# Making the inner sums of the image for q and k of the second pair on VectorE instead of loading them

## The chip, the cores and the metric

One core of one Trainium2 chip. The metric is the device time of one execution in microseconds (us), the median of several executions.

## The reference, cut to what matters

An attention block on x of shape (16, 512, 32, 32), fp32, four heads of 128 channels, 1024 positions:

```python
    xn = group_norm(x, 8 groups) * gamma + beta
    qkv = jnp.einsum('oc,bchw->bohw', qkv_w, xn) + qkv_b[:, None, None]
    q, k, v = jnp.split(qkv, 3, axis=1)
    # ... to heads ...
    attn = jax.nn.softmax(jnp.einsum('bhnd,bhmd->bhnm', q, k) * scale, axis=-1)
    out = jnp.einsum('bhnm,bhmd->bhnd', attn, v)
    # ... back to channels ...
    out = jnp.einsum('oc,bchw->bohw', proj_w, out) + proj_b[:, None, None]
    return x + out
```

## The kernel before

The products for q, k, v and the projection are two-level Strassen products (7 of 8 block products, twice). The inner level needs four sums of image blocks, t1 to t4, for each of four groups of outer products. The image is the same for the first pair of heads, for v and for the second pair, so before made the sums once ("keep": made on VectorE, stored to DRAM) and loaded them twice ("load"):

```python
            def load(h, m):
                if sums == "load" and h < len(OUTER):
                    nc.sync.dma_start(sum_tile(h, m), inner_kept[b, h, m])

            def inner_sum(m):
                if sums == "load":
                    return
                sum_tile(g, m)
                a, c = {
                    "t1": ("b12", "b11"), "t2": ("b22", "t1"), "t3": ("t2", "b11"),
                    "t4": ("b21", "t2"),
                }[m]
                for i in range(n):
                    nc.vector.tensor_sub(have[m][:, i, :], inner(i, a), inner(i, c))
                if sums == "keep":
                    ...  # stored by GpSimd's queue
```

Scores (s), exponentials (p) and the weighted sum (po) of one head run beside one such product. In head 0 of a batch that is q and k of the second pair, in head 1 the projection of the batch before, in head 2 q and k of the first pair of the next batch, in head 3 its v. The softmax denominators of the head before are summed on VectorE, their reciprocals written to DRAM as one row and read back broadcast to all partitions, and the division waits for that:

```python
    def denominators(b, h):
        ...
        nc.vector.reciprocal(r, l[:, 3, :])
        row = dpool.tile([1, N], F32, tag="row", name=f"row_{b}_{h}")
        nc.sync.dma_start(row.rearrange("o (c i) -> (o c) i", i=BLK), r)
        rinv[b, h] = lpool.tile([P, N], F32, tag="rinv", name=f"rinv_{b}_{h}")
        nc.sync.dma_start(rinv[b, h], row.to_broadcast((P, N)))
    ...
    def divide(b, h):
        nc.vector.tensor_mul(os_[b, h], os_[b, h], rinv.pop((b, h)))
```

v is transposed through DRAM, by GpSimd's queue: each finished block is written (vd<-vu) and read back in four parts of 128 KB (v<-vd). The last of these reads fall into head 0 of the next batch.

## Time and profile before

| | before |
|---|---|
| median of 3 executions | 3350.72 us (3336.61 to 3360.77) |
| TensorE, VectorE busy | 96%, 75% of the span |
| heads 0, 1, 2, 3, mean of batches 1 to 14 | 56.2, 50.0, 51.2, 49.2 us |
| bytes moved | 589.27 MB |

TensorE is busy almost throughout, so the question is only where it stands. The four kinds of head need about equal matmul work, yet head 0 is 5 to 7 us longer than the others, and the list of waits has one large entry there, on an addition that frees the y bank, the accumulator that the next product needs (L529). That addition stands on VectorE behind the division, and the division waits for the broadcast of the reciprocals. The prediction shows the lines. The view that names the end of that chain is VectorE's list of waits (us in total, times, longest us), of before:

```profile
DVE o L807 <- DMA rinv<-row: 129.0, 36, 9.8
```

### The profile page before, as it was taken

To read this page: it belongs to the slowest core of one execution; us is meant where nothing else is said; L and a number is where in the kernel's file an instruction comes from. 1 tells how busy PE (TensorE), PEld (TensorE's weight loads), DVE (VectorE), ACT (ScalarE), POOL (GpSimd) and SP (SyncE) were. 2 spreads that over 40 slices of the span, in tenths; PEclk is the share of its full clock that TensorE was granted. 3 is DMA by queue.
4 is the path that set the end of the run, shared out by engine and by line. 5 is a ranking of instruction groups with operands and counts; after the bars stand their busy time and mean duration, and the time that the engine had idled before them with its cause. 6 is when DMAs were issued, how large, how long until landed. Compare 5 with 4: busy or idle time off the path is not lost.

```text
span 3343.7 us, 33635 instructions
## 1 busy us (share of the span) xinstructions
PE 3216.1 (96%) x10474; PEld 2183.1 (65%) x10474; DVE 2521.0 (75%) x4161; ACT 1437.4 (43%) x2709; POOL 525.6 (16%) x938
## 2 busy tenths in 40 slices
PE   8999999999999999999999999999999999999999
PEld 6566666666666666666666666666666666666664
DVE  7876868768687776877768677786777868778675
ACT  2534435344353443535435353353534435344342
POOL 1011121111211112120121201212012121121100
PEclk9999999999999999999999999999999999999999
DMA  6665564555645456464564645646456464464731
GB/s 222 218 202 174 171 211 148 180 174 176 214 157 183 156 184 200 160 189 152 178 197 160 193 150 179 211 148 211 141 170 212 154 215 141 162 202 161 219 128 45
DMA packets 209527, 589.27 MB, mean 176 GB/s; under 512 B 32960, under 2 KB 64192, under 8 KB 209344
## 3 DMA queue, kind: packets, MB, share of 16 engines
q1 hardware_dynamic: 140080, 368.89, 34.1%
q0 software_dynamic: 67392, 216.07, 19.2%
q10 hardware_dynamic: 1872, 2.11, 0.2%
q8 instruction: 86, 1.41, 0.2%
q14 instruction: 97, 0.79, 0.1%
HBM read 448.28 MB, written 138.67 MB: 176 GB/s over the span
## 4 chain that ended last, share of the span: by engine, by line
PE 57%; DVE 11%; issue 9%; DMA 9%; POOL 1%; ACT 0%; POOLq 0%; DVEq 0%; SPq 0%; ACTq 0%
PE po L797 16%; PE s L712 15%; PE qk_x L510 6%; PE qk_y L510 5%; PE v_x L510 4%; PE pp_x L510 3%; PE v_y L510 3%; PE pp_y L510 3%; DMA w<-kept 2%; DMA rinv<-row 2%; DMA y<-in_x 2%; DMA row<-r 2%; DVE xt L272 1%; DVE tot L725 1%; DVE vt L649 1%
## 5 line engine op out<-in xcount | busy, mean ns | idle before, releaser
L717 ACT ACTIVATE p<-s 128x512 f32<-128x512 f32 x1024 | 610.1, 596 | 1069.4 <-PE s L712 1063.8
L712 PE MATMUL s<-qk,qk 128*128 128x512 f32 x2048 | 1060.2, 599 | 2.2 <-ACT p L717 1.9
L797 PE MATMUL po<-p,v 128*128 128x512 f32 x2048 | 1058.4, 598 | 1.3 <-ACT o L804 1.3
L797 PEld LDWEIGHTS po<-p,v 128*128 128x128 f32 x2048 | 602.1, 303 | 331.8 <-issue 215.5
L725 DVE TENSOR_TENSOR tot<-tot,p 128x1024 f32<-128x1024 f32 x385 | 469.8, 1220 | 115.2 <-ACT p L717 112.7
L712 PEld LDWEIGHTS s<-qk,qk 128*128 128x128 f32 x2048 | 391.8, 192 | 93.7 <-issue 29.7
L510 PEld LDWEIGHTS qk_x<-qk_t,w 128*128 128x128 f32 x1344 | 251.1, 191 | 180.9 <-issue 71.9
L510 PE MATMUL qk_x<-qk_t,w 128*128 128x256 f32 x1344 | 360.5, 385 | 7.2 <-ACT qk_u L421 5.9
L529 DVE TENSOR_TENSOR qk_r<-qk_y,qk_u 128x512 f32<-128x512 f32 (+1 forms) x256 | 158.8, 620 | 158.3 <-ACT qk_u L421 132.6
L421 ACT COPY qk_u<-qk_x 128x512 f32<-128x512 f32 (+1 forms) x256 | 136.1, 532 | 254.2 <-PE qk_x L510 254.2
L499 POOL DMA_DIRECT2D kept_t<-qk_t x256 | 138.2, 541 | 487.8 <-DVE qk_t L495 439.8
L510 PE MATMUL qk_y<-qk_t,w 128*128 128x256 f32 x448 | 135.5, 418 | 72.4 <-DVE qk_r L529 67.4
L660 POOL DMA_DIRECT2D vd<-vu x120 | 66.3, 552 | 804.6 <-DVE vu L652 780.3
L807 DVE TENSOR_TENSOR o<-o,rinv 128x1024 f32<-128x1024 f32 x63 | 77.0, 1223 | 129.5 <-DMA rinv<-row 129.0
L510 PE MATMUL pp_x<-pp_t,w_proj 128*128 128x256 f32 x630 | 173.3, 389 | 0.0
L510 PEld LDWEIGHTS v_x<-v_t,w_v 128*128 128x128 f32 x630 | 118.4, 190 | 79.1 <-issue 38.3
L697 POOL DMA_DIRECT2D out_y<-y x120 | 66.2, 551 | 652.1 <-DVE y L696 619.8
L529 DVE TENSOR_TENSOR v_r<-v_y,v_u 128x512 f32<-128x512 f32 (+1 forms) x120 | 74.7, 623 | 124.2 <-ACT v_u L421 116.6
L510 PE MATMUL v_x<-v_t,w_v 128*128 128x256 f32 x630 | 166.6, 381 | 0.0
L510 PEld LDWEIGHTS qk_y<-qk_t,w 128*128 128x128 f32 x448 | 87.1, 203 | 113.2 <-DVE qk_r L529 73.3
L665 POOL DMA_DIRECT2D v<-vd x240 | 139.9, 590 | 100.6 <-issue 45.2
L510 PEld LDWEIGHTS pp_x<-pp_t,w_proj 128*128 128x128 f32 x630 | 113.9, 190 | 63.7 <-issue 18.9
(204 smaller groups left out, 4358.4 us busy)
## 6 DMA issues: line engine op xcount, KB each, us to landing
w<-kept SPq DMA_DIRECT2D x90, 896.0 KB, 6.3
kept_t<-qk_t POOLq DMA_DIRECT2D x192, 256.0 KB, 2.9
qk_t<-kept_t SPq DMA_DIRECT2D x192, 256.0 KB, 4.6
v_t<-kept_t SPq DMA_DIRECT2D x180, 256.0 KB, 2.7
w_v<-kept_v SPq DMA_DIRECT2D x45, 896.0 KB, 4.9
w_proj<-kept_proj SPq DMA_DIRECT2D x45, 896.0 KB, 4.5
rinv<-row SPq DMA_DIRECT2D x63, 512.0 KB, 4.9
x<-in_x POOLq DMA_DIRECT2D x60, 512.0 KB, 5.6
```

Of the source, the lines that this page charges most:

```text
L421: nc.scalar.copy(t[n][:, :width], t["x"][:, :width])
L499: nc.gpsimd.dma_start(t, have[m][:, :n])
L510: nc.tensor.matmul(acc[:, ts(i, Q)], have["w"][:, i, SLOTS[an], :], inner(i, bn), start=(first and i == 0), stop=True, skip_group_check=True,)
L529: nc.vector.tensor_add(dst, view(a), view(c))
L660: nc.gpsimd.dma_start(rows[which][ts(h, P), :], u)
L665: nc.gpsimd.dma_start(vs[b, pair][ts(q, BLK), half].rearrange("m h (k i) j -> m (h k) (i j)", k=n), rows[which].rearrange("(k m) (q e) -> ...
L697: nc.gpsimd.dma_start(out[b, ts(o, P), ts(half, HALF)], t)
L712: nc.tensor.matmul(sc, ks[b, h][:, ts(j, P)], qs[b, h][:, ts(half, HALF)], start=True, stop=True)
L717: nc.scalar.activation(ps[s][:, ts(half, HALF)], sc, AF.Exp, scale=SCALE)
L725: nc.vector.tensor_add(tot[b, h][:, i], tot[b, h][:, i], ps[s][:, i])
L797: nc.tensor.matmul(po[b, h][:, i], v_block(b, h, j), ps[s][:, i], start=(j == 0), stop=(j == NB - 1),)
L807: nc.vector.tensor_mul(os_[b, h], os_[b, h], rinv.pop((b, h)))
```

## The change

The intent is to spend VectorE's spare time in head 0 in place of loads there. q and k of the second pair make their sums ("make") and store nothing; v alone loads the stored ones.

```diff
         return two_levels(
-            f"qk_{b}_{pair}", pair, b, lambda: xb[b], finish, "load" if pair else "keep"
+            f"qk_{b}_{pair}", pair, b, lambda: xb[b], finish, "make" if pair else "keep"
         )
@@
     next_v, next_qk = [], [qk_groups(0, 1)]
-    ahead["qk_0_1"]()
@@
-                units.append(ahead[f"v_{b + 1}" if h == 2 else f"qk_{b + 1}_1"])
+                if h == 2:
+                    units.append(ahead[f"v_{b + 1}"])
```

## The prediction

> **What bounds the kernel now.** I began with the page of the whole execution, which names the busiest engine, and then cut the span at the first score matmul (s) of each head, because four kinds of head alternate and have different limits. In head 0 of a batch the scores run beside q and k of the second pair (the part that the change touches), in head 1 beside the projection of the batch before, in head 2 beside q and k of the first pair of the next batch, in head 3 beside its v.
>
> ```profile
> PE 3216.1 (96%) x10474; PEld 2183.1 (65%) x10474; DVE 2521.0 (75%) x4161; ACT 1437.4 (43%) x2709; POOL 525.6 (16%) x938
> ```
>
> TensorE is the bound, VectorE (DVE) second at 75%. The table of stretches for batch 7, heads 0, 1, 2, 3, in this order:
>
> ```profile
> core 0: us, PE busy (x) PEld busy (x) DVE busy (x) ACT busy (x) POOL busy (x), PEclk, DMA share, GB/s
> 1487.00:1543.20 56.20, 51.02 (x164) 34.77 (x163) 36.06 (x54) 19.02 (x34) 12.43 (x22) 0.97 0.69 211
> 1543.20:1593.60 50.40, 49.80 (x168) 34.33 (x167) 42.45 (x80) 33.48 (x70) 7.29 (x12) 1.00 0.36 125
> 1593.60:1644.70 51.10, 49.74 (x163) 33.50 (x162) 43.48 (x78) 19.13 (x34) 9.70 (x18) 1.00 0.54 184
> 1644.70:1694.00 49.30, 49.05 (x164) 34.27 (x164) 35.19 (x49) 19.13 (x34) 5.09 (x9) 1.00 0.57 184
> ```
>
> Head 0 is the long one: 56.2 us (14 such heads, batches 1 to 14, sum to 787.3 us, mean 56.2; heads 1, 2 and 3 average 50.0, 51.2 and 49.2). Its clock is below 1.00 and its DMA share is the highest, while its VectorE load is one of the two lowest. All four need about the same matmuls: in the timeline two records of 512 columns start 0.86 us after the two before, and so do four of 256, so 64 and 98 of them take 64 x 0.43 + 98 x 0.215 = 48.6 us. Head 0 thus loses 7.6 us per batch, the others 0.6 to 2.6. The list of TensorE's waits over the span names the loss:
>
> ```profile
> PE qk_y L510 <- DVE qk_r L529: 67.9, 15, 7.9
> PE qk_x L510 <- DMA w<-kept: 18.4, 23, 2.1
> ```
>
> 15 waits, one per batch, mean 4.5 us. The timeline of batch 7, VectorE:
>
> ```profile
> 1494.59 0.17 DVE L739 TENSOR_TENSOR l<-l 32x32 f32<-32x32 f32 x1
> ...
> 1495.46 0.34 DVE L742 RECIPROCAL r<-l 32x32 f32<-32x32 f32 x1
> ...
> 1499.68 1.22 DVE L723 TENSOR_TENSOR tot<-p,p 128x1024 f32<-128x1024 f32 x1 [1.69 <-ACT p L717]
> 1507.62 1.23 DVE L807 TENSOR_TENSOR o<-o,rinv 128x1024 f32<-128x1024 f32 x1 [6.72 <-DMA rinv<-row]
> ...
> 1511.42 0.68 DVE L529 TENSOR_TENSOR qk_r<-qk_y,qk_u 128x512 f32<-128x512 f32 x1
> ```
>
> TensorE:
>
> ```profile
> 1505.73 1.03 PE L510 MATMUL qk_x<-qk_t,w 128*128 128x256 f32 x4
> 1511.56 1.87 PE L510 MATMUL qk_y<-qk_t,w 128*128 128x256 f32 x4 [4.80 <-DVE qk_r L529]
> 1513.22 1.91 PE L712 MATMUL s<-qk,qk 128*128 128x512 f32 x2
> ```
>
> The queue of SyncE (SP):
>
> ```profile
> 1493.23 0.32 SPq L484 DMA_DIRECT2D qk_t<-kept_t  x1
> 1495.83 0.32 SPq L744 DMA_DIRECT2D row<-r  x1
> 1496.25 0.51 SPq L484 DMA_DIRECT2D qk_t<-kept_t  x1
> 1500.77 0.32 SPq L746 DMA_DIRECT2D rinv<-row  x1
> 1501.19 0.86 SPq L484 DMA_DIRECT2D qk_t<-kept_t  x2
> 1504.21 0.32 SPq L350 DMA_DIRECT2D w<-kept  x1
> ```
>
> The chain: reciprocal done at 1495.8; the 4 KB row goes out at once, but the broadcast that reads it is issued only 4.9 us later and lands another 6.8 us later. VectorE stands 6.72 us at the division, and the additions that free the y bank are behind it, so TensorE stands 4.80 us. Then s takes 1.91 instead of 1.02 us: half clock, about 1.8 us more.
>
> **What the Trainium skill says.** (1) "TensorE: Matmul & The Clock Gate", Part 1: after about one idle window of 3.4 us the array drops to half rate, and the window is free-running. The trace agrees (the 1.91 us above), except that in batch 4 an idle of 2.64 us was enough. (2) The same page, on the array and the queue depths: ACT and DVE are strict FIFO; that is why a late broadcast holds additions that are ready. (3) "DMA: Bandwidth & Descriptors", "Issuing engines are not separate DMA queues": SP's and GpSimd's transfers share 16 engines. The trace agrees: in stretches of 4 us the DMA share is 0.97 to 1.05 from 1503 to 1519. (4) "VectorE: DVE Perf Modes", on the errata and the tier table: fp32 tensor_tensor runs at 1x, 58 + 256 cycles at 0.96 GHz, 0.33 us. Records of this form last 0.41 us but start 0.335 us apart back to back, so the cost is the page's.
>
> **The change, part by part.** It removes per batch the 12 loads of 256 KB and 4 of 128 KB of head 0, 3.5 MB, 56 MB of 589. (The stores stay, v loads them.) It adds 28 subtractions per batch:
>
> ```profile
> L495 DVE TENSOR_TENSOR qk_t<-x,qk_t 128x256 f32<-128x256 f32 x128 | 51.6, 413 | 0.6
> ```
>
> 28 x 0.335 = 9.4 us of VectorE per batch, 150 us in all. Head 0 goes from 36.1 to about 46 us of VectorE, against 43.5 in head 2, which makes the same sums today and loses 2.6 us.
>
> Now TensorE's path in head 0, with the order of the changed kernel on batch 7's times. *First wait.* One t1 subtraction comes ahead of the last v outputs, in a stretch where VectorE has no gap: it delays the end of v by 0.33 us. The second t1 stands behind L739: it starts at 1494.65 and ends at 1495.07. TensorE, which now takes s between the two halves of that product, wants it at 1493.46: 1.6 us lost. The two t2 follow behind the small transpose and behind the reciprocal, ending at 1495.6 and 1496.3, where a full TensorE would have needed them earlier: with the restart the product with t2 ends at 1496.8 and not 1494.75, so 2.05 us are lost. No single idle reaches 2.6 us, so I expect no clock drop. *Division.* The reciprocal moves only to 1495.55. Without the two loads around it I put the row at 2.5 us (over the trace the row lands in 2.1 by the median, and here the v transfers still run) and the broadcast at 5 us (median 4.9): landing at 1504. VectorE reaches the division at 1502.3, after the first tot, and has 1.13 (it) + 0.67 (two t4) + 1.25 (two L272) + 1.2 (two L529) = 4.25 us until the bank is free, 1508.3. TensorE, 2 us late, arrives at 1508.0. So 0.3 us, in place of 4.8, and no half clock. *Weights of group 2.* Their load (w) is issued when group 0 ends (1505.4) and needed 6.3 us later. In head 2 they land in 5.5 to 6.1, in head 0 today in 10.5, hidden by the long wait. With the sums' loads gone but x and residuals still loading, I choose 7: 0.7 us. *Rest* of the head, small releases and restarts: 0.9 us. Sum: 2.05 + 0.3 + 0.7 + 0.9 = 4.0 us, against 7.6: 3.6 us saved.
>
> Total: 15 batches x 3.6 = 54 us; less 15 x 0.33 = 5 at the end of v; less an estimated 2 in batch 0, where head 0 loses only 1.0 today and VectorE gets fuller. Net 47: 3350.7 - 47 = 3304 us, 1.4% faster.
>
> **Rivals.** *A, head 0 becomes head 2*: 51.2 us, 5.0 saved, 75 in all, less 7: 3283 us, just at 2%. For it: same matmuls, same sums. Against: head 0 starts behind v's transposes and a division, and the t2 come late by the order. *B, the wait stays*: v's transfers of GpSimd (eight v<-vd issued from 1499 to 1503) and not the loads keep the broadcast late, while the first wait is added: about 4.8 + 1.8 + 2 remain, 3350 to 3370. For it: engines stay full through v's part even without 3.5 MB. Against: two loads stand in the very queue of row and broadcast. *C, VectorE becomes the bound in head 0*: 46 of 52.6 us is 88%, and single waits for bank y come back; each 2.6 us wait would also cost the clock. That gives 3320 to 3350. Against: heads 1 and 2 run at 85% with 1.4 and 2.6 us of loss, and VectorE idles 20 of 56.2 us in head 0 today.
>
> **Range and chances.** The middle is 3303. Rivals A and C bound it: 3270 to 3338. The threshold of 2% is 3284, only reached if nearly all of A comes true: 0.23. Slower than 3418 needs more than B: 0.03. Within 2%: 0.74.
>
> **What would show it.** Right: head 0 at 52 to 53 us; the list of waits loses the 67.9 us of qk_y on L529 and gains some 25 us of waits on qk_t subtractions; the gap before the division (6.72 us in batch 7) falls to about 2; the clock in head 0 is 1.00; weights wait up to 1 us more per batch. Wrong: row and broadcast as late as now (B), or new waits on L529 through the second half of head 0 (C), or no early wait (A).

## The result, and the profile after

After: 3314.73 us, median of 4 executions (3313.17 to 3319.11), against 3349.2 of before (4 executions, 3336.61 to 3360.77). The ratio is 0.99, 95% interval 0.9863 to 0.9937. Ratios here are the mean time of one kernel's runs over that of the other's of the same rounds, so not quite the ratio of the medians quoted. The kernel is 1.0% faster by the ratio, 34.5 us by the medians.

The page's first part, of after: 448 more instructions on VectorE, 139 us more busy time, TensorE's work unchanged.

```profile
PE 3206.6 (97%) x10474; PEld 2169.8 (65%) x10474; DVE 2659.6 (80%) x4609; ACT 1437.6 (43%) x2709; POOL 525.5 (16%) x938
```

The heads now take 53.98, 50.00, 51.30 and 49.42 us (before 56.22, 50.02, 51.20, 49.25; means of batches 1 to 14, cut at each head's first score matmul in the trace). 14 batches save 14 x 1.99 = 27.9 us; batches 0 and 15 and the start lose 1.5; together the 26.4 us by which the two profiled spans differ (3343.7 and 3317.3). Only head 0 gains. The stretch of head 0 in batch 7 of after (span, busy time of each engine, clock, DMA share, GB/s), whose heading the prediction shows:

```profile
1479.30:1534.30 55.00, 50.97 (x164) 34.58 (x163) 44.61 (x81) 18.95 (x34) 12.43 (x22) 0.97 0.54 161
```

The DMA share fell from 0.69 to 0.54 and VectorE rose from 36.06 to 44.61 us, but the clock is still 0.97. TensorE's waits over the span of after:

```profile
PE qk_y L510 <- DVE qk_r L529: 36.9, 16, 5.1
PE qk_y L510 <- DVE qk_t L495: 29.2, 27, 1.8
PE qk_x L510 <- DMA w<-kept: 11.5, 17, 1.6
```

The wait behind the division was halved (67.9 to 36.9 us), not removed, and a new wait on the subtractions came (qk_t; 22.0 of the 29.2 us in heads 0 of batches 1 to 15). VectorE's list of waits of after:

```profile
DVE o L807 <- DMA rinv<-row: 100.4, 39, 8.7
```

Batch 7 of after shows both waits. VectorE:

```profile
1486.90 0.40 DVE L495 TENSOR_TENSOR qk_t<-x 128x256 f32<-128x256 f32 x1
...
1487.64 0.33 DVE L742 RECIPROCAL r<-l 32x32 f32<-32x32 f32 x1
...
1493.20 1.23 DVE L723 TENSOR_TENSOR tot<-p,p 128x1024 f32<-128x1024 f32 x1 [0.30 <-ACT p L717]
1498.97 1.23 DVE L807 TENSOR_TENSOR o<-o,rinv 128x1024 f32<-128x1024 f32 x1 [4.54 <-DMA rinv<-row]
```

TensorE:

```profile
1487.35 0.70 PE L510 MATMUL qk_y<-qk_t,w 128*128 128x256 f32 x2 [1.46 <-DVE qk_t L495]
...
1502.85 2.07 PE L510 MATMUL qk_y<-qk_t,w 128*128 128x256 f32 x4 [2.57 <-DVE qk_r L529]
1504.72 1.65 PE L712 MATMUL s<-qk,qk 128*128 128x512 f32 x2
```

SyncE's queue, with no load of sums left in it (the last line merges two issues, so its 17.60 us is no transfer time):

```profile
1488.00 0.32 SPq L744 DMA_DIRECT2D row<-r  x1
1490.57 0.32 SPq L746 DMA_DIRECT2D rinv<-row  x1
1497.73 17.60 SPq L350 DMA_DIRECT2D w<-kept  x2
```

GpSimd's queue:

```profile
1487.82 0.54 POOL L684 DMA_DIRECT2D y<-in_x  x1
1488.65 4.06 POOL L665 DMA_DIRECT2D v<-vd  x7 [0.29 <-issue]
1493.21 0.58 POOL L665 DMA_DIRECT2D v<-vd  x1 [0.50 <-DMA v<-vd]
```

In the means of batches 1 to 14 the row now lands sooner (issued 8.73 us into head 0, landed 2.09 us later; before 8.95 and 4.76), so the broadcast is issued 2.9 us earlier, at 10.8 us. But it then takes 8.4 us to land (before 6.6), at 19.2 us into the head (before 20.3). Of the 2.9 us, 1.8 are given back in the transfer. In batch 7 seven reads of v are issued around it and one behind them. The second idle of TensorE there, 2.57 us, again costs the clock: the two s after it take 1.65 us and not 1.02. Of the 14 heads 0, the clock is 1.00 in 6 and 0.97 in 8.

### The profile page after: what moved, and what is told of

It reads as the page before. It is cut to its first block, busy times and chain, and to the rows that moved or that the text cites.

```text
span 3317.3 us, 33461 instructions
## 1 busy us (share of the span) xinstructions
PE 3206.6 (97%) x10474; PEld 2169.8 (65%) x10474; DVE 2659.6 (80%) x4609; ACT 1437.6 (43%) x2709; POOL 525.5 (16%) x938
## 3 DMA queue, kind: packets, MB, share of 16 engines
q0 software_dynamic: 67392, 216.07, 20.3%
## 5 line engine op out<-in xcount | busy, mean ns | idle before, releaser
L510 PE MATMUL qk_y<-qk_t,w 128*128 128x256 f32 x448 | 132.7, 403 | 64.2 <-DVE qk_r L529 34.8
L529 DVE TENSOR_TENSOR qk_r<-qk_y,qk_u 128x512 f32<-128x512 f32 (+1 forms) x256 | 158.7, 620 | 41.7 <-ACT qk_u L421 22.0
L529 DVE TENSOR_TENSOR v_r<-v_y,v_u 128x512 f32<-128x512 f32 (+1 forms) x120 | 74.8, 623 | 124.8 <-ACT v_u L421 117.1
L510 PEld LDWEIGHTS pp_x<-pp_t,w_proj 128*128 128x128 f32 x630 | 113.8, 190 | 63.9 <-ACT pp_u L421 18.9
L665 POOL DMA_DIRECT2D v<-vd x240 | 139.9, 590 | 53.3 <-issue 44.7
```

The lines of the kernel that those rows point to most:

```text
L510: nc.tensor.matmul(acc[:, ts(i, Q)], have["w"][:, i, SLOTS[an], :], inner(i, bn), start=(first and i == 0), stop=True, skip_group_check=True,)
L529: nc.vector.tensor_add(dst, view(a), view(c))
L665: nc.gpsimd.dma_start(vs[b, pair][ts(q, BLK), half].rearrange("m h (k i) j -> m (h k) (i j)", k=n), rows[which].rearrange("(k m) (q e) -> ...
```

## The experiments

My theory before the first run: the broadcast lands late because the reads of v share the DMA engines with it, and the first wait (on t1) is a loss beside it. The rivals: the first wait alone bounds head 0, or VectorE does. Over all runs I measured the same things in the trace, means of batches 1 to 14:

| kernel | row lands after issue | broadcast lands after issue | lands, us into head 0 | head 0, us | median, us | ratio to before [95%] |
|---|---|---|---|---|---|---|
| before | 4.8 | 6.6 | 20.3 | 56.2 | | |
| after | 2.1 | 8.4 | 19.2 | 54.0 | 3314.73 | 0.99 [0.9863, 0.9937] |
| e1, no sums at all | 3.8 | 6.6 | 19.4 | 55.2 | 3335.88 | 0.9959 [0.9939, 0.9978] |
| e4, division later | 2.1 | 8.1 | 18.9 | 52.2 | 3298.31 | 0.9843 [0.9826, 0.9859] |
| e6, before, division later | 4.7 | 6.4 | 19.9 | 56.7 | 3355.65 | 1.0014 [0.9993, 1.0034] |
| e5, reads of v held | 2.0 | 6.1 | 16.9 | 51.1 | 3280.12 | 0.979 [0.9774, 0.9806] |
| e5 again | 2.1 | 6.1 | 16.9 | 51.0 | 3279.41 | 0.9817 [0.98, 0.9833] |
| e7, before, reads held | 4.3 | 6.3 | 19.5 | 55.6 | 3345.45 | 0.9985 [0.9952, 1.0018] |
| e3, group 0 loaded | 3.7 | 5.6 | 18.1 | 53.5 | 3326.62 | 0.9934 [0.9906, 0.9962] |
| e9, group 0 loaded, reads held | 3.8 | 5.6 | 18.2 | 53.3 | 3324.9 | 0.9919 [0.9895, 0.9943] |
| e10, end of v later | 1.5 | 5.6 | 16.6 | 51.5 | 3277.62 | 0.9808 [0.9791, 0.9824] |
| e11, end of v later, reads held | 1.5 | 5.9 | 17.1 | 51.0 | 3272.99 | 0.9803 [0.9784, 0.9822] |
| e14, reads of c21 held | 1.9 | 7.8 | 18.4 | 52.5 | 3301.21 | 0.9867 [0.9845, 0.989] |
| e15, reads of c12 held | 2.0 | 6.7 | 17.4 | 51.2 | 3277.22 | 0.9798 [0.9775, 0.9821] |

Before ran beside them: 3350.98 us (7 runs) with e1, e4, e5, e6; 3349.67 (9) with e3, e7, e9; 3341.88 (7) with e10, e11 and e5 again; 3342.0 (7) with e14, e15.

### e1_no_sums: neither loaded nor made

The second pair reads raw blocks in place of sums. The result is wrong (relative error 0.10).

```diff
             def inner_sum(m):
-                if sums == "load":
+                if sums == "load" or site == 1:
                     return
@@
             def inner(i, m):
+                if m[0] == "t" and site == 1:
+                    m = {"t1": "b12", "t2": "b22", "t3": "b22", "t4": "b21"}[m]
```

> Wrong result on purpose: the second pair's q and k neither load nor make their inner sums, every product reads raw image blocks instead. My theory: in head 0 the first wait (1.6 us, on the t1 subtraction) goes, but TensorE then reaches the held y bank about 2 us earlier, and the division still stands until the broadcast lands, some 19 us into the head; so the wait on L529 grows from 2.3 to about 4 us per batch, the clock drops in nearly every batch, and the time stays at 3305 to 3320. Rival, that the subtractions cost what their waits show (29 us) on top: about 3285.

Measured: 3335.88 us, slower than after. TensorE's waits of this kernel (its L531 is the addition L529):

```profile
PE qk_y L512 <- DVE qk_r L531: 64.0, 16, 5.2
```

Both times missed, but the mechanism of my theory came: without the first wait TensorE comes to the division earlier, the broadcast lands at 19.4 us (after: 19.2), the wait there is back at 64.0 us, some 4 us per batch, and the clock drops in all 14 heads 0. So removing the first wait gained nothing here; it lies in the shadow of the broadcast. The row took 3.8 us here with no loads of sums left, so these loads are not all that makes it late. It was issued 0.44 us behind a load of the residual in most batches, where after issues it 0.18 us behind; that this is the reason is not shown.

### e4_late_division and e6_before_late_division: the division behind a later addition

In head 0 the division is put behind the running sum of step 3, in after (e4) and in before (e6), so that the additions that free the bank no longer stand behind it.

```diff
                 if half == 0 and j == 5 and s > NB:
-                    divide(*where(s - NB)[:2])
+                    if h == 0:
+                        with tc.issue_after(tot_add[s - 2].ins):
+                            divide(*where(s - NB)[:2])
+                    else:
+                        divide(*where(s - NB)[:2])
```

> The changed kernel with only the division of head 0 moved: VectorE may take it only after the running sum of step 3. My theory: the wait of TensorE on L529 in head 0 (37 us) and the half clock (some 15 us) go, head 0 falls from 54.0 to about 52 us, its clock is 1.00, the time is about 3282 (3274 to 3292). Rival, that another wait (weights of group 2, or VectorE as the bound) takes its place: 3300 or more.

> The kernel before with only the division of head 0 moved as in the run above it. If the held division were all that the change relieved, head 0 would fall from 56.2 to about 50 us and the time to 3255 to 3270, below every kernel that makes the sums. My theory: the loads also keep the weights of group 2 late (10.5 us from issue to landing against 6.3 us until they are wanted), so a wait on these of about 4 us, with half clock after it, comes in its place: 3295 to 3330.

e4: 3298.31 us, between the two expectations. The wait on L529 in head 0 is gone, but the weights of group 2 are met:

```profile
PE qk_x L510 <- DMA w<-kept: 32.5, 28, 2.4
```

e6: 3355.65 us, no gain, and my number missed. But the mechanism of my theory came: nearly all of the wait moved to the weights (66.4 us in heads 0, with half clock in all 14 of batches 1 to 14), which land 10.8 us after their issue while the sums are loaded (counted from the end of the issuing instruction, as are all landings of weights here):

```profile
PE qk_x L510 <- DMA w<-kept: 81.4, 30, 6.3
```

So in before two things lay under the wait, one behind the other, and removing the upper alone gains nothing. In e4 the weights land 6.5 us after their issue, and 16.8 us of waits on them are left in heads 0. Moving the division pays only after the loads of sums are gone.

### e5_v_held: the last eight reads of v wait for the division

```diff
+            if which in ("c21", "c12"):
+                held.append(read)      # the four dma_start of v<-vd, as a function
+            else:
+                read()
@@
     def divide(b, h):
-        nc.vector.tensor_mul(os_[b, h], os_[b, h], rinv.pop((b, h)))
+        ins = nc.vector.tensor_mul(os_[b, h], os_[b, h], rinv.pop((b, h)))
+        while held and h == HEADS - 1:
+            held.pop(0)(ins)           # each read depends on the division
```

> The changed kernel, but the last eight reads of v (v<-vd, GpSimd's queue) wait for the division of head 0. If these eight are why the broadcast takes 8.2 us in head 0, it lands within 5.5 us of its issue, the gap before the division falls from 4.2 to under 1.5 us, the waits on L529 nearly vanish, and the time is about 3288 (3278 to 3300), unless the reads, now later, delay something else. Rival, that residual and image loads or the broadcast itself are slow: landing still 7 us or more, 3310 to 3320.

Measured: 3280.12 us, correct, 0.979: inside the range given, though the landing took 6.1 us and not 5.5. The division in batch 7, and the reads behind it in GpSimd's queue:

```profile
1479.58 1.23 DVE L823 TENSOR_TENSOR o<-o,rinv 128x1024 f32<-128x1024 f32 x1 [1.29 <-DMA rinv<-row]
```

```profile
1481.10 4.65 POOL L668 DMA_DIRECT2D v<-vd  x8 [6.61 <-DVE o L823]
```

The gap before the division is 1.29 us, where after has 4.54. The broadcast lands at 16.9 us, the waits on L529 fall to 3.8 us in all heads 0, and the clock is 0.999. The hold also moves what GpSimd's queue, which runs in order, has behind the reads: the loads of x go out some 10 us later (24.1 us and not 14.6), and loads of the residual earlier. So it is not the reads alone that moved.

### e7_before_v_held: the same hold without the change

The edit of e5, on before.

> The kernel before (sums loaded), with the last eight reads of v held until the division of head 0, as in the run that held them in the changed kernel. If v's reads alone made the broadcast late, the loads would cost nothing once these are held: 3275 to 3290, and the change would be worth nothing on top. My theory: loads and reads of v compete for the same engines in the same 20 us, so either alone keeps the row or the broadcast late: row still lands some 4 us after its issue, division at 18 to 19 us into head 0, waits on L529 of 25 to 50 us over the run, 3305 to 3325.

Measured: 3345.45 us, 0.9985; both expectations missed, mine in size: the waits on L529 stay at 60.3 us and not 25 to 50. The row still lands 4.3 us and the broadcast 6.3 us after their issue. The change alone is worth 35 us, the hold alone about 4 (its interval includes nothing), the two together some 70. With the loads of sums or with the reads of v, either alone, the broadcast stays past 19 us.

### e3_first_loaded and e9_first_loaded_v_held: only group 0 loaded

The sums of group 0 are loaded again at the end of head 3, those of groups 1 to 3 made, so that no subtraction stands ahead of the reciprocal and the first wait goes. e9 has the hold of e5 too. The edit is shown against before, whose loads ahead of group 0 stay:

```diff
-                if sums == "load":
+                if sums == "load" or (sums == "first" and g == 0):
                     return
@@
-            f"qk_{b}_{pair}", pair, b, lambda: xb[b], finish, "load" if pair else "keep"
+            f"qk_{b}_{pair}", pair, b, lambda: xb[b], finish, "first" if pair else "keep"
```

> The changed kernel, but the sums of the first group of the second pair are loaded as before (at the end of head 3) and only those of the other groups made. My theory: the first wait on a subtraction (22 us over the heads 0) goes, but as in the run without sums TensorE comes to the y bank 2 us earlier, while the broadcast lands as late as ever, so the wait on L529 grows to about 60 us and the clock drops in most batches: 3320 to 3338, slower than the changed kernel. Rival, that the first wait is a cost by itself: about 3290.

> As the run with the first group loaded, and the last eight reads of v held until the division. My theory: now that the broadcast lands by about 17 us, nothing stands behind the first wait and its removal counts: head 0 falls from 51.1 us to 49.4 to 50.2, waits on L529 stay under 12 us over the run, 3250 to 3268, faster than every kernel so far. Rival, that the earlier TensorE just meets the division again: 3275 to 3290.

e3: 3326.62 us, inside the range, but with 39.8 us of waits on L529 and not about 60, as the broadcast lands at 18.1 us and not as late as ever. e9: 3324.9 us (5 rounds), a clear miss. The first wait went in both, yet with the reads held the division is met as long as without. Waits of e9:

```profile
PE qk_y L510 <- DVE qk_r L529: 42.7, 16, 4.7
```

With 1 MB of loads at the seam of the two heads the row lands 3.7 us after its issue again, and the whole chain with it (18.2 us). That the loads do it is argued: the order on VectorE changed too, and e1 has a late row without them.

### e10_v_tail_later and e11_v_tail_and_held: the other order at the seam

t1 and t2 of group 0 are made before the denominators' work, and the last additions, writes and reads of v are emitted after it. e10 removes and holds no transfer; e11 adds the hold of e5.

```diff
                 if g == len(OUTER) - 1:
-                    run(pending)
+                    if site == "v":
+                        tail.extend(pending)
+                    else:
+                        run(pending)
                     pending.clear()
@@
         if 0 < s < steps and s % NB == 0:
+            if h == 0:
+                ahead[f"qk_{b}_1_make"]()      # t1, t2 of group 0
             denominators(*where(s - 1)[:2])
+            run(tail)
+            tail.clear()
```

> The kernel after, with the order on VectorE at the seam of head 3 and head 0 changed: the first two subtractions t1 and t2 come before the denominators' work, and the last additions of v with their writes and reads come after it. No transfer is removed. My theory: the first wait (1.6 us a batch on t1) goes, but the broadcast of the reciprocals still lands at about 19 us into head 0 because the reads of v share the engines with it, so TensorE only arrives about 1.6 us earlier at the same landing: waits for the division 50 to 65 us in all instead of 37, half clock in most heads 0, 3310 to 3335 us. Rival: the first wait is what bounds head 0; without it head 0 is some 2 us shorter, about 3285 to 3295 us.

> The same, and the last eight reads of v wait for the division of head 0, as in the run in which only they were held (3280 us). My theory: with the broadcast landing at about 17 us the first wait counts, so removing it brings head 0 from 51.1 us to 49.5 to 50.5: 3255 to 3275 us, waits for the division under 12 us in all. Rival: the division is met again as soon as TensorE comes 1.6 us earlier: waits for the division 20 to 30 us, 3275 to 3290 us, no better than holding the reads alone.

e10: 3277.62 us. My theory missed by over 30 us, and the rival's range lies a little above it too. The row is issued later, at 9.6 us, but lands in 1.5, and the broadcast lands after 5.6 us though six reads of v are issued during its transfer: at its issue 3.1 transfers with 0.53 MB are under way on average, where after has 4.2 with 0.68 MB, among them a load of the residual (which now goes out at 18.8 us and not 8.6). Waits of e10:

```profile
PE qk_x L512 <- DMA w<-kept: 23.6, 28, 2.0
PE qk_x L512 <- DVE qk_t L497: 11.7, 16, 1.2
PE qk_y L512 <- DVE qk_r L531: 10.4, 6, 2.6
```

e11: 3272.99 us, inside my range at its upper end, but not by my reason: head 0 takes 51.0 us and not 49.5 to 50.5, the waits for the division are 13.1 us and not under 12, and the ratio cannot be told from that of e5 on the same chip (0.9803 and 0.9817, the intervals overlap). The rival, the division is met again, describes it better, with its size too large. Waits of e11:

```profile
PE qk_y L512 <- DVE qk_r L531: 13.1, 14, 3.2
PE qk_x L512 <- DVE qk_t L497: 11.6, 16, 1.2
```

The wait on the subtractions went from 1.47 us a head to about 0.7, and what TensorE gained came back at the division: in heads 0, e5 again waits 22.0 + 3.0 us on these two, e11 10.4 + 12.8. So with an early broadcast too the first wait is worth nothing measurable. Heads 0 are at 51.0 us in both.

> The best kernel so far, once more on this chip, so that it can be compared with the two others under the same conditions: 3275 to 3286 us, ratio 0.977 to 0.981, waits for the division 3 to 6 us in all.

The repeat of e5 gave 3279.41 us, its own number again, but a ratio of 0.9817, a little above the range; before was faster on that chip.

### e14_c21_held and e15_c12_held: which half of the hold

c21 and c12 are the two blocks of v's product that are finished last; each is read in four parts. Only one condition of e5 is changed: `if which == "c21"` (e14) and `if which == "c12"` (e15).

> The kernel after, with only four of the eight reads of v held until the division: those of block c21, which in the kernel after are issued 7.9 to 10.8 us into head 0, before the broadcast (10.9 us). The four of c12, issued at 11.4 to 13.5 us, stay. My theory: what stands in the engines' queues ahead of the broadcast delays it, so this half of the hold has nearly all the effect: landing 6 to 6.8 us after its issue instead of 8.4, waits for the division 5 to 12 us in all, 3279 to 3292 us. Rival: all transfers under way share the engines alike, whether issued before or after: half the effect, landing about 7.2 us, 3292 to 3303 us.

> The other half: only the four reads of c12, issued after the broadcast, are held. My theory: nearly no effect, landing 7.6 to 8.4 us after the issue, waits for the division 25 to 37 us in all, 3303 to 3317 us. Rival (sharing, whether issued before or after): half the effect, landing about 7.2 us, 3292 to 3303 us.

Measured: 3301.21 us for e14, with the broadcast landing after 7.8 us, and 3277.22 us for e15, with 6.7. Each is the reverse of what my theory said. The rival's range holds the time of e14 but not that of e15, and both its landings (7.2) are off. Waits of e14, then of e15:

```profile
PE qk_y L510 <- DVE qk_r L529: 22.8, 14, 3.8
```

```profile
PE qk_y L510 <- DVE qk_r L529: 7.8, 11, 2.5
```

Holding the reads of c12 has nearly all of the effect of e5. Holding those of c21 shortens the landing by 0.6 us, where e5 shortens it by 2.2, but head 0 by 1.5 of e5's 2.9 us, as the clock now drops in 1 of the 14 heads 0 and not in 8. By the ratios e14 can't be told from after. But neither run moves four reads alone. In e14 two loads of the residual move up into the place of the held reads (9.3 and 9.9 us), and the reads of c12 move up too (to 10.9 to 12.7 us, from 11.6 to 13.7). So 0.79 MB are still under way when its broadcast is issued (after: 0.68), and e14 does not test what an empty queue ahead would give. In e15 the loads of x wait behind the held reads (21.5 us and not 14.6). It has 0.65 MB under way at the issue and lands in 6.7 us; e5 has 0.79 MB, as e14 has, and lands in 6.1. So what stands ahead of the broadcast does not by itself set its landing; and e10, where six reads are issued during the broadcast and it still lands in 5.6 us, speaks against equal sharing with whatever is issued later.

## Why the prediction was right or wrong

The time was right: 3303 predicted, range 3268 to 3338, measured 3314.73, within 2% as held most likely. By its steps:

**First wait: right.** 1.6 us predicted, 22.0 / 15 = 1.47 measured (batches 1 to 15); the waits on qk_t grew from 4.6 to 29.2 us, and some 25 were expected. No clock was lost by it. That it adds to the head's loss was wrong: e1, e9 and e11 remove or halve it and gain nothing, though in e1 and e9 the row is late as well. The end of v lost 0.17 us per batch (head 3), not 0.33.

**Division: the mechanism was right, its size off; this is the term that failed.** The row came as predicted (2.5 us; measured 2.1), and so did the issue. The broadcast was put at 5 us, the median of all broadcasts of the trace, most of which run in emptier heads, and took 8.4. So it landed at 19.2 us into the head and not at 17. The 0.3 us of wait became 34.8 / 15 = 2.3 us per head, with half clock in 8 heads of 14 where none was expected. The limit used for the clock was wrong too, no drop below an idle of 2.6 us: the clock fell after idles of 1.91 us (batch 13) and 1.97 us (batch 4), and not after 2.27 us (batch 1); even in before one of 2.49 us (batch 12) was enough. That reading of rival B, v's transfers keep the broadcast late, was half true, and its number was not: the row's gain stayed. Two slips did little: by the lines shown TensorE stopped at 1506.76, so 2 us late is 1508.8 and not 1508.0; and of the 15 waits on L529 only 14 are of head 0, the last is 0.5 us elsewhere.

**Weights of group 2: right in size, absent as a loss.** They land 6.85 us after their issue (7 chosen, by the same count), but TensorE is late by the division and does not meet them; the waits on weights even fell from 18.4 to 11.5 us. e4, where the division is out of the way, meets them.

**The sum.** 4.0 us of loss were predicted for head 0, 52.6 us; measured 53.98, hence 35 us gained and not 47. The predicted landing of 17 us was reached by e5, and there head 0 takes 51.0 and not 52.6, a loss of 2.4 us: the first wait and 0.9 us of rest. So without the miss on the broadcast the sum would have been too pessimistic; first wait, weights and rest were put side by side in full, where they partly hide each other. That the total came so near is in part luck: two errors of opposite sign.

**Rivals.** A (head 0 becomes like head 2, 51.3 us) is what e5, e10, e11 and e15 reach, 51.0 to 51.5 us and 3273 to 3280 us. C, VectorE as the bound, found no support: the same 44.6 us of VectorE in head 0 fit into 50.65 us in e5's batch 7.

What the table shows most clearly is that, wherever the division stands in its old place, head 0 follows the landing of the broadcast more than anything else. Landing at 16.6 to 17.4 us gives 51.0 to 51.5 us, 18.1 to 18.4 gives 52.5 to 53.5, 19.2 to 19.5 gives 54.0 to 55.6, 20.3 gives 56.2. It holds from batch to batch too: over the 14 heads 0 the landing and the length of the head go together with a correlation of 0.95 in before and 0.91 in after, but 0.02 in e4, where the division is out of the way. At about equal landing the kernels without the first wait are no shorter: e9 (18.2 us) takes 53.3 us, with half clock in 9 heads of 14, and e14, which has the wait (18.4 us), 52.5, with half clock in 1. The change, the hold and the order at the seam all move this landing.

**What stays open** is which transfers around the broadcast delay it, and by what rule. Neither what is issued ahead (e5, e15) nor equal sharing (e10) explains all runs, and the holds move other loads of the same queue. A count of the trace's packet records shows what the engines did meanwhile: between issue and landing they moved 1.83 MB in after, 1.76 in e14, 1.46 in e5, 1.35 in e10, of which 0.52 MB is the broadcast, and they were busy for 97, 84, 69 and 93% of that time. Between the first and the last of the broadcast's 128 packets, GpSimd's queue moved 154 packets of the same size in after, in 5.31 us, and 68 in e10, in 3.09 us; but 141 in e11, in 3.58 us, so this alone is no rule either. Why the row lands sooner in after is open as well: e1, without loads of sums, has it late (3.8 us). Whether e10, e11, e5 and e15 differ from each other is open too; their intervals overlap. All four beat both kernels by an interval that excludes after's.

## What to carry to other kernels

Find the small transfer on which the slow stage hangs (here one row and its broadcast), read its landing in that very stage rather than its median over the trace, and ask what else is moved at that time. Try two removals together before you drop one: here the change gained 35 us, the hold of v's reads alone next to nothing, and both together 70. A wait that lies in the shadow of a later one is worth nothing by itself: take it away in an experiment before you count it.

## What the Trainium skill lacked or had wrong

- "DMA: Bandwidth & Descriptors", "Queues, rings and completion order": it says that each engine takes turns between the queue rows that have work, packet by packet. It gives no way to tell what a transfer on one row loses to another. Here the 512 KB broadcast took 5.6 to 8.4 us in the same stage, and in after 1.83 - 0.52 = 1.31 MB of other data went through meanwhile, over twice its own size.
- "TensorE: Matmul & The Clock Gate", Part 1: the idle window of about 3.4 us is no safe limit. In batch 7 of after an idle of 2.57 us was followed by half clock (two s in 1.65 us and not 1.02), and in batch 13 one of 1.91 us was enough, while one of 2.27 us in batch 1 was not followed by it.
